# Neighbour sums in pairs in the scores' PSUM tiles, and the pieces of k over both other banks

## The chip, the cores and the metric

The kernel runs on one core of a Trainium2 chip. Times are device microseconds (us) of that core. Each time is a median of several executions. The traces' spans are some 2 us shorter than the times. Tables count batches from 1; the code counts them from 0. PE is TensorE's matmul, PEld its weight load, DVE VectorE, ACT ScalarE, POOL GpSimd.

## The reference

Two layers over x of 32 batches, 512 nodes, 512 features, all in fp32:

```
layer 0:  x = layernorm(x + deg * (x Wi' + b) + A (x Wj'))        A: the 512 x 512 graph, deg: its row sums
layer 1:  q, k, v = projections of x;  8 heads of 64
          x = layernorm(x + softmax(mask(q k' / 8)) v Wo' + bo)
```

## The kernel before

The program is a recorded list of pieces. While a batch n is in attention, eight steps each issue scores for four heads and a quarter of the keys, then the values (attention times v) of the step before, then other work: layer 0 of batch n+1, projections, the neighbour sums (`l0_gather`, x' A') of the batch after. Pieces are given weights and cut into the steps by these (`by_steps`).

PSUM has eight banks, and all are taken: one bank each for `mma` and `mmb`, two for `ov`, and two `sc` tiles of two banks each.

```python
def mm_tile(bank):
    return psum.tile([P, 512], FT, name="mm" + bank, bufs=1)
def sc_tile():
    return psum.tile([P, 2, N], FT, name="sc", bufs=2)
...
def l0_gather(b, dc, bank, adjT=None):
    ...
    pm = mm_tile(bank)
    parts = SPLIT.pop((b, dc))                    # xhi, xlo: x in two parts of type fp32r
    for w in range(2):
        for jc in range(NC):
            nc.tensor.matmul(pm, parts[w][:, jc, :], adjR[:, jc, :], start=..., stop=...)
    nc.scalar.copy(AX_T[b][:, dc, :], pm)         # ACT takes it out of PSUM
    if adjT is None and dc + 2 < DC:
        split(b, dc + 2)                          # ACT cast, POOL subtraction
...
def base(b, half):                                # DVE: y += deg * b0, two SBUF inputs
    for ic in range(2 * half, 2 * half + 2):
        y = XT[b][:, ic, :]
        nc.vector.scalar_tensor_tensor(y, b0_r, deg_c[:, ic:ic + 1], y, op0=OP.mult, op1=OP.add)
...
def scores(b, hp, kc):
    ps = sc_tile()
    ...                                           # matmuls, exp on ACT in place
    nc.vector.tensor_tensor(e, ps, edge..., op=OP.mult)   # the mask: last reader of ps
```

A gather is eight matmuls of 512 columns in fp32r, a second number type of TensorE. A piece of k is four matmuls of 256 columns in fp32, into a bank that DVE then adds into k. The trace lists an fp32 matmul twice and an fp32r matmul once, so a piece of k shows as eight records, x8; it prints both types as f32.

## Time and profile before

| | before |
|---|---|
| time, median of 5 | 3709.78 us (3708.73 to 3709.93) |
| span in the trace | 3706.9 us |
| PE busy | 3665.2 us, 99% |
| DVE, POOL, ACT busy | 65%, 53%, 28% |
| one batch in attention, start to start | 113.43 us |
| first scores, from the span's start | 117.45 us |

PE is busy nearly throughout, so the kernel is as long as its chain of matmuls. A batch's duration is the difference between the starts of its first scores and those of the next batch, in the timeline of PE; it is the same within 0.01 us from batch 2 to batch 30.

### The profile page before, as it was taken

To read this page: it belongs to the slowest core of one execution; us is meant where nothing else is said; L and a number is where in the kernel's file an instruction comes from. 1 tells how busy PE (TensorE), PEld (TensorE's weight loads), DVE (VectorE), ACT (ScalarE), POOL (GpSimd) and SP (SyncE) were. 2 spreads that over 40 slices of the span, in tenths; PEclk is the share of its full clock that TensorE was granted. 3 is DMA by queue.
4 is the path that set the end of the run, shared out by engine and by line. 5 is a ranking of instruction groups with operands and counts; after the bars stand their busy time and mean duration, and the time that the engine had idled before them with its cause. 6 is when DMAs were issued, how large, how long until landed. Compare 5 with 4: busy or idle time off the path is not lost.

```text
span 3706.9 us, 49623 instructions
## 1 busy us (share of the span) xinstructions
PE 3665.2 (99%) x18458; PEld 2511.4 (68%) x18458; DVE 2396.9 (65%) x3139; ACT 1029.1 (28%) x1482; POOL 1946.5 (53%) x1986
## 2 busy tenths in 40 slices
PE   8999999999999999999999999999999999999997
PEld 5666666666676767676666767676767666666763
DVE  4566766666666666666666666666666666666666
ACT  2222232222322222323233222222232332222322
POOL 3465545555455564455554555644555545556443
PEclk9999999999999999999999999999999999999999
DMA  7444556455555545554555544455545555445541
GB/s 250 125 126 133 151 151 162 124 141 138 152 159 145 128 135 150 153 160 120 141 142 154 159 141 130 134 151 157 157 122 139 141 159 157 137 132 137 151 131 44
DMA packets 797174, 530.02 MB, mean 143 GB/s; under 512 B 530433, under 2 KB 611841, under 8 KB 796929
## 3 DMA queue, kind: packets, MB, share of 16 engines
q1 hardware_dynamic: 780384, 494.78, 49.4%
q10 hardware_dynamic: 16320, 31.46, 2.3%
q8 instruction: 151, 2.47, 0.3%
q14 instruction: 95, 0.77, 0.1%
q0 software_dynamic: 224, 0.53, 0.0%
HBM read 453.25 MB, written 73.40 MB: 142 GB/s over the span
## 4 chain that ended last, share of the span: by engine, by line
PE 96%; DVE 1%; SPq 1%; POOL 1%; DMA 0%; issue 0%; ACT 0%; POOLq 0%; DVEq 0%; ACTq 0%
PE mma L427 31%; PE mmb L427 31%; PE sc L481 13%; PE ov L503 13%; PE mmb L325 3%; PE mma L325 3%; PE sc L513 2%; SPq L113 0%; DMA wv<-e 0%; DVE e L486 0%; DVE rl L522 0%; DVE st L289 0%; SPq L144 0%; PE sc L721 0%; SPq L166 0%
## 5 line engine op out<-in xcount | busy, mean ns | idle before, releaser
L485 ACT ACTIVATE sc<-sc 128x1024 f32<-128x1024 f32 x512 | 493.1, 1006 | 1538.4 <-PE sc L481 1532.2
L486 DVE TENSOR_TENSOR e<-sc,edge 128x1024 f32<-128x1024 f32 x512 | 602.5, 1218 | 211.4 <-ACT sc L485 180.4
L427 PE MATMUL mmb<-ring,big 128*128 128x256 f32 x3144 | 733.7, 382 | 3.1 <-issue 3.1
L427 PE MATMUL mma<-ring,big 128*128 128x256 f32 x3112 | 724.5, 381 | 3.9 <-ACT p L434 2.8
L427 PEld LDWEIGHTS mmb<-ring,big 128*128 128x128 f32 x3144 | 593.7, 190 | 134.1 <-issue 30.2
L427 PEld LDWEIGHTS mma<-ring,big 128*128 128x128 f32 x3112 | 585.7, 190 | 135.6 <-issue 27.0
L481 PE MATMUL sc<-q,k 64*128 64x512 f32 x2048 | 509.7, 616 | 0.0
L396 POOL TENSOR_TENSOR big<-big 128x512 f32<-128x512 f32 x376 | 493.1, 1339 | 29.3 <-ACT big L354 10.1
L503 PE MATMUL ov<-e,v 128*32 128x512 f32 x4096 | 494.0, 600 | 3.6 <-DVE oT L538 3.6
L492 POOL TENSOR_TENSOR es<-e 128x1024 f32<-128x1024 f32 x128 | 301.0, 2364 | 346.0 <-DVE e L486 346.0
L427 PE MATMUL mma<-big,ring 128*128 128x256 f32 x1808 | 431.5, 382 | 3.2 <-DVE k L465 3.2
L427 PE MATMUL mmb<-big,ring 128*128 128x256 f32 x1776 | 422.7, 381 | 0.0
L291 POOL TENSOR_SCALAR mv<-mv 128x1 f32<-128x1 f32 x256 | 51.0, 199 | 672.5 <-DVE mv L290 660.0
L427 PEld LDWEIGHTS mma<-big,ring 128*128 128x128 f32 x1808 | 341.0, 190 | 76.8 <-issue 25.1
L427 PEld LDWEIGHTS mmb<-big,ring 128*128 128x128 f32 x1776 | 334.5, 190 | 72.0 <-issue 25.1
L503 PEld LDWEIGHTS ov<-e,v 128*32 128x32 f32 x4096 | 107.1, 109 | 351.6 <-issue 321.7
L204 POOL TENSOR_TENSOR xlo<-xh,xhi 128x512 fp32r<-128x512 f32 x128 | 164.0, 1294 | 337.3 <-ACT xhi L203 337.2
L481 PEld LDWEIGHTS sc<-q,k 64*128 64x128 f32 x2048 | 176.5, 186 | 208.4 <-issue 205.4
L340 POOL TENSOR_TENSOR big<-big,deg_r 128x512 f32<-128x512 f32 x124 | 174.0, 1404 | 266.5 <-DVE big L339 266.5
L494 DVE TENSOR_TENSOR es<-es,e 128x1024 f32<-128x1024 f32 x251 | 307.7, 1227 | 0.0
L445 DVE TENSOR_TENSOR xh<-xh,mma 128x512 f32<-128x512 f32 x186 | 126.7, 681 | 269.7 <-PE mma L427 269.7
L445 DVE TENSOR_TENSOR xh<-xh,mmb 128x512 f32<-128x512 f32 x186 | 126.7, 681 | 262.6 <-PE mmb L427 262.6
(147 smaller groups left out, 3659.5 us busy)
## 6 DMA issues: line engine op xcount, KB each, us to landing
ring<-wo SPq DMA_DIRECT2D x217, 256.0 KB, 2.8
ring<-wq SPq DMA_DIRECT2D x160, 256.0 KB, 3.9
ring<-wv SPq DMA_DIRECT2D x160, 256.0 KB, 3.3
ring<-wk SPq DMA_DIRECT2D x160, 256.0 KB, 3.4
ring<-wi SPq DMA_DIRECT2D x155, 256.0 KB, 2.7
ring<-wj SPq DMA_DIRECT2D x155, 256.0 KB, 2.6
xh<-in_x_dram SPq DMA_DIRECT2D x32, 1024.0 KB, 5.5
xa<-in_x_dram SPq DMA_DIRECT2D x124, 256.0 KB, 3.9
```

Source lines behind the costliest of these rows:

```text
L204: nc.gpsimd.tensor_sub(lo, xs, hi.bitcast(FT))
L325: nc.tensor.matmul(pm, parts[w][:, jc, :], adjR[:, jc, :], start=(w == 0 and jc == 0), stop=(w == 1 and jc == NC - 1))
L340: nc.gpsimd.tensor_tensor(XD[b][:, dc, :], XD[b][:, dc, :], deg_r, op=OP.mult)
L396: nc.gpsimd.tensor_tensor(dst, p, q, op=OP.subtract)
L427: nc.tensor.matmul(pm[:, c * Q:(c + 1) * Q], lhs, rhs, start=first, stop=(kc == 1 and n == len(terms) - 1), skip_group_check=True)
L445: nc.vector.tensor_tensor(d, d, pm, op=OP.add)
L481: nc.tensor.matmul(ps[:, s, :], KT[b, hp // 2][r, hp % 2, kc * P:(kc + 1) * P], QT[b, hp // 2][r, hp % 2, :], start=True, stop=True)
L485: nc.scalar.activation(ps, ps, AF.Exp, scale=QSCALE)
L486: nc.vector.tensor_tensor(e, ps, edge[:, kc:kc + 1, :].to_broadcast([P, 2, N]), op=OP.mult)
L492: nc.gpsimd.tensor_add(ES[i], E[i, 0], E[i, 1])
L494: (eng or nc.vector).tensor_add(ES[i], ES[i], E[i, kc])
L503: nc.tensor.matmul(PV[g][r][32 * h:32 * h + 32, :], V[b][:, kc, c0:c0 + 32], E[h // 2, kc][:, h % 2, :], start=(kc == 0), stop=(kc == NC - 1))
```

## The change

Its intent: put two neighbour sums behind one another, in the two halves of one scores tile, so that their bank is free and the pieces of k can alternate between two banks.

```diff
-        pm = mm_tile(bank)
+        if bank == "sc":
+            if dc % 2 == 0:
+                OPEN["gather"] = sc_tile()
+            pm = OPEN["gather"][:, dc % 2, :]
+        else:
+            pm = mm_tile(bank)
...
-        g = [(GA, l0_gather, n, dc, A) for dc in range(DC)]
-        k = [pc("k", n - 1, i, K) for i in LATE]
-        res = []
-        for i in range(DC):
-            res += g[i:i + 1] + k[i:i + 1] + [z(l0_turn, n, i)]
-            if i in (1, 2):
-                res += [z(base, n, i - 1)]
-            if n == 1 and i in (1, 3):
-                res += [z(combine, "wo", nc.vector, i // 2)]
-            if i == 1:
-                res += [z(combos, TX, n, xq, (1,)), z(combos, TA, n, aq, (1,))]
+        g = [(GA, l0_gather, n, dc, "sc") for dc in range(DC)]
+        k = {i: pc("k", n - 1, i, A if i in (5, 3) else K) for i in LATE}
+        wo = [z(combine, "wo", nc.vector, i) for i in range(2)] if n == 1 else [z(base, n, 0), z(base, n, 1)]
+        res = [g[0], g[1], k[5]] if n == 1 else [k[5], g[0], g[1]]
+        res += [z(l0_turn, n, 0), k[6], z(l0_turn, n, 1), z(combos, TX, n, xq, (1,)), z(combos, TA, n, aq, (1,)), k[3], wo[0],
+                k[7], wo[1], g[2], g[3], z(l0_turn, n, 2), z(l0_turn, n, 3)]
+        if n == 1:
+            res += [z(base, n, 0), z(base, n, 1)]
```

(The return that follows is only broken over its lines in another way.)

More of the change, by code (lines that the diff above doesn't have):

```diff
@@ L571, in phase_a @@
         xq, aq = lambda j, m: quarter(XD[n], j, m), lambda j, m: quarter(AX_T[n], j, m)
-        g = [(GA, l0_gather, n, dc, A) for dc in range(DC)]
-        k = [pc("k", n - 1, i, K) for i in LATE]
-        res = []
-        for i in range(DC):
-            res += g[i:i + 1] + k[i:i + 1] + [z(l0_turn, n, i)]
-            if i in (1, 2):
-                res += [z(base, n, i - 1)]
-            if n == 1 and i in (1, 3):
-                res += [z(combine, "wo", nc.vector, i // 2)]
-            if i == 1:
-                res += [z(combos, TX, n, xq, (1,)), z(combos, TA, n, aq, (1,))]
+        g = [(GA, l0_gather, n, dc, "sc") for dc in range(DC)]
[6 more added lines that the diff above has]
+            res += [z(base, n, 0), z(base, n, 1)]
         return res + [z(combos, TX, n, xq, (2,)), z(combos, TA, n, aq, (2,)),
-                      z(combos, TX, n, xq, (3, 4)), z(combos, TA, n, aq, (3, 4)),
-                      pc("l0", n, 1, A), k[4]]
+                      z(combos, TX, n, xq, (3, 4)), z(combos, TA, n, aq, (3, 4)), pc("l0", n, 1, A), k[4]]
     def first():
```

## The prediction

> **What bounds the kernel now.** I read the page from the top: busy shares, then the chain that ended last.
>
> ```profile
> PE 3665.2 (99%) x18458; PEld 2511.4 (68%) x18458; DVE 2396.9 (65%) x3139; ACT 1029.1 (28%) x1482; POOL 1946.5 (53%) x1986
> ...
> PE 96%; DVE 1%; SPq 1%; POOL 1%; DMA 0%; issue 0%; ACT 0%; POOLq 0%; DVEq 0%; ACTq 0%
> ```
>
> TensorE (PE) is busy for all but 3706.9 - 3665.2 = 41.7 us of the span, and 96% of the last chain is matmuls. The chain in order of time repeats its entries every 113.43 us (1008.76, 1122.19, 1235.62): one batch, with the same pattern each time. So there is almost no idle PE to win. What can change is how long the matmuls take where they change from one kind to another, or a new wait in each batch. I therefore went to the timeline of PE, over the stretch where the changed code runs.
>
> ```profile
> 986.45 1.99 PE L481 MATMUL sc<-q,k 64*128 64x512 f32 x8
> 988.37 1.92 PE L503 MATMUL ov<-e,v 128*32 128x512 f32 x16
> 990.23 1.21 PE L325 MATMUL mmb<-adjR,xhi 128*128 128x512 f32 x4
> 991.27 1.07 PE L325 MATMUL mmb<-adjR,xlo 128*128 128x512 f32 x4
> 992.18 1.89 PE L427 MATMUL mma<-big,ring 128*128 128x256 f32 x8
> 993.72 1.28 PE L325 MATMUL mmb<-adjR,xhi 128*128 128x512 f32 x4
> 994.84 1.08 PE L325 MATMUL mmb<-adjR,xlo 128*128 128x512 f32 x4
> 995.75 1.89 PE L427 MATMUL mma<-big,ring 128*128 128x256 f32 x8
> ...
> 1001.14 1.99 PE L481 MATMUL sc<-q,k 64*128 64x512 f32 x8
> 1003.06 1.92 PE L503 MATMUL ov<-e,v 128*32 128x512 f32 x16
> 1004.91 1.21 PE L325 MATMUL mmb<-adjR,xhi 128*128 128x512 f32 x4
> 1005.96 1.07 PE L325 MATMUL mmb<-adjR,xlo 128*128 128x512 f32 x4
> 1006.87 1.89 PE L427 MATMUL mma<-big,ring 128*128 128x256 f32 x8
> 1008.59 3.62 PE L427 MATMUL mmb<-ring,big 128*128 128x256 f32 x16
> 1012.05 1.89 PE L427 MATMUL mma<-big,ring 128*128 128x256 f32 x8
> ```
>
> The first column is the start, so differences of starts are what each piece costs. A neighbour sum (gather) is the pair of L325 lines, a piece of k is eight L427 matmuls. From 1006.87 to 1008.59 eight plain matmuls take 1.72 us, from 1008.59 to 1012.05 sixteen take 3.46 us: 0.216 us each, 1.73 for eight. A gather has eight matmuls too, but k piece and gather together, 992.18 to 995.75, take 3.57 us, not 3.46: going into the fp32r form and out again costs about 0.12 us. A gather right behind the values (L503) takes 1.96 us, 0.23 over. A k piece there would take 1.83 us: 0.10 over (I read that behind other values lines, 1061.54 to 1063.37).
>
> The second view is the same stretch on DVE and POOL, in front of the scores that start at 1001.14:
>
> ```profile
> 999.31 1.27 POOL L340 TENSOR_TENSOR big<-big,deg_r 128x512 f32<-128x512 f32 x1
> 999.39 3.42 DVE L345 SCALAR_TENSOR_TENSOR xh<-b_r,deg_c,xh 128x512 f32<-128x512 f32 x2 [0.21 <-POOL xlo L204]
> 1000.66 3.28 POOL L396 TENSOR_TENSOR big<-big 128x512 f32<-128x512 f32 x2
> ...
> 1002.72 0.68 DVE L465 TENSOR_TENSOR k<-mma,k 128x512 f32<-128x512 f32 x1
> 1003.36 2.35 DVE L486 TENSOR_TENSOR e<-sc,edge 128x1024 f32<-128x1024 f32 x2
> ```
>
> The two base additions (L345) take 1.7 us each here, beside POOL; by themselves such an instruction takes 0.70 us (the group's minimum 705 ns, median 1746). They delay L465 and then the masking e<-sc (L486), which is the last reader of a scores tile.
>
> **What the Trainium skill says.** "SBUF — State Buffer", section "Who interferes with whom": a DVE instruction with two SBUF inputs and a GpSimd instruction that reads SBUF share an interface, and the second to issue blocks until the first has finished. The trace agrees: 0.70 against 1.75 us, and L345 ends about 0.55 us after the POOL operation that it overlapped (999.31 + 1.27 = 1000.58; the first L345 ends at 1001.13). "Perfetto Trace Analysis", section "Matmuls": independent groups should rotate through PSUM banks so that the eviction of one overlaps the next. The kernel before does that by alternating gather (one bank) and k piece (the other), and its PE shows no gap there; so the change cannot win hidden evictions. "TensorE: Matmul & The Clock Gate", section "Step-by-step: what each phase is for": a stream costs its N columns per matmul, with the drain hidden. The 0.216 us for 256 columns agree with two passes of 256 at 2.4 GHz plus 2.5 ns, which is my estimate from that page.
>
> **The change part by part.** Instructions are neither added nor removed: the program order has 2054 rows on PE before and after. (a) A batch had four separate gathers, each between other work; now there are two pairs, each in the two halves of a scores tile. (b) Pieces 5 and 3 of k go to the bank that the gathers left, 6, 7, 4 stay in the other. The built order of one batch is now: scores, values, k5, g0 g1, k6, k3, k7, scores, values, g2 g3, 16 matmuls of l0, k4. (c) On DVE the first base now stands between the additions of k3 and k7, where before it stood ahead of one k addition; the second base still comes behind the masks.
>
> PE, from the first values to the next batch's scores. Before: 1013.87 - 988.37 = 25.50 us. After, from the same starts: values 1.85, k5 1.64 (the first fp32r matmul starts 0.19 earlier than a plain one would), first pair 1.12 + 0.86 + 0.86 + 0.91 = 3.75, k6 1.73, k3 1.73, k7 1.82 (to scores), scores 1.92, values 1.85, second pair 1.96 + 1.73 = 3.69, l0 3.46, k4 1.82. Sum 25.26. The gain is 0.24 us a batch, two changes of kind fewer. Thirty batches have this under attention, and the preparation of batch 1 has it once more: 31 x 0.24 = 7.4 us.
>
> New waits. The first pair needs the third scores tile, that is the first of the two of this step, after its mask. With k5 ahead of it there is 1.6 us to spare: no wait. The second pair follows the values directly, 3.77 us (1.92 + 1.85) after the scores start, so the first mask of the step must have ended by then. Before, it ended at 1003.36 + 1.22 = 1004.58, which is 3.44 after the scores: 0.33 to spare. After, I work it out with the scores of the first step at 0. k6 runs 9.16 to 10.89, k3 to 12.62, k7 to 14.35, second scores at 14.43. POOL: the copy of g1 at 9.37, its fp32r cast 0.48 later, xlo 0.70 later at 10.55 to 11.85, then the two L340 to 13.1 and 14.34, then L396. DVE: addition of k3 at 12.82 (0.2 after its matmuls), base at 13.44, in the middle of the second L340. Its first half ends at 14.34 + 0.55 = 14.89, POOL's next ends at 16.02 (it starts late by 0.32), the second half at 16.57; addition of k7 from 16.49, mask from 17.12 to 18.34. That is 3.91 after the scores, 0.47 later than before. Waiters on this mask (L513) started 0.05 after it, so the gather would start at 3.96 in place of 3.77: 0.19 us lost a batch, 30 x 0.19 = 5.7 us.
>
> Net: -7.4 + 5.7 = -1.7 us; 3709.2 - 1.7 = about 3707.5. I take 3707, as the wait may be partly hidden.
>
> **The rivals.** (1) No wait at all: the base falls between POOL operations, or the lock is granted otherwise. Then the whole 7.4 us stay: 3702. For it speaks that 0.19 us rests on a chain of ten durations; against it that POOL has a queue of four operations just there. (2) A longer wait: one more POOL operation comes before the base, and the mask ends a whole L340 (1.27 us) less some slack later. A wait of 0.5 us a batch is 30 x 0.5 = 15 less 7.4: about 3717. (3) k7 waits for the DVE read of k6, which now has only k3 between them (1.73 us) in place of a gather and more: the two additions of k6 start at 11.1 and end at 11.99, k7 starts at 12.62, 0.6 to spare; only a late DVE makes this a wait. (4) DMA: three k pieces now take their weights within 5.2 us. Seven ring tiles and 2.7 to 3.9 us to landing make this safe.
>
> **Range and chances.** All of these are under 0.5% of the time, and 2% is 74 us, or 2.4 us a batch, which none of them reaches. The range goes from no wait with a slightly larger gain (3700) to a wait of some 0.4 us a batch (3714). Faster by over 2%: 0.01; within: 0.98; slower: 0.01.
>
> **What would show it.** In the PE timeline of after: the first pair should stand between two k pieces at about 3.75 us from start to next start; the batch should repeat every 113.43 - 0.24 + 0.19 = 113.4 us. The gather behind the second values should be named as waiting for the mask e<-sc, with the start some 3.9 to 4.0 us after the scores; if it stands at 3.77, rival 1 is right. The base pair on DVE should still take about 3.1 us beside POOL; with 1.4 the lock argument has failed. A wait of k7's weights on the k addition would be rival 3. I would be wrong altogether if another engine or the ring got gaps over 2 us in each batch.

## More of the kernel before

`combine("wo", ...)` is five DVE operations, done once per program, for n == 1 in the code, which is ahead of the first scores.

## The result

The changed kernel took 3771.76 us (median of 5, 3770.03 to 3773.24), 62 us more. The ratio to before is 1.0169, 95% interval 1.0155 to 1.0183; a ratio here is the mean time of one kernel's fast runs over that of the other's in the same rounds, so not quite the quotient of the medians. The results are correct. The prediction of 3707 us, 3700 to 3714, was wrong.

The page of the changed kernel, busy shares and the last chain by engine:

```profile
PE 3685.2 (98%) x18458; PEld 2505.1 (66%) x18458; DVE 2357.2 (63%) x3139; ACT 1029.3 (27%) x1482; POOL 1933.4 (51%) x1986
...
PE 95%; DVE 1%; ACT 1%; SPq 1%; POOL 1%; issue 0%; DMA 0%; DVEq 0%; POOLq 0%; ACTq 0%
```

The span is 63.0 us longer (3769.9 against 3706.9), but PE's busy time only 20 us. PE now idles 43 us more, and ACT has come into the chain with 1%, where it had 0%. The view of waits, with the total in us, the number of waits and the longest, names them:

```profile
PEld sc L331 <- ACT big L337: 66.2, 60, 1.1
...
PE sc L331 <- ACT big L337: 40.5, 60, 0.7
```

L331 is the gather's matmul and L337 the copy of a gather out of PSUM. Sixty gathers wait for a copy; in the kernel before three did, 0.7 us together (PE), all in the first batch's layer 0. PEld (66.2 us) and PE (40.5 us) describe one and the same wait, so they aren't added. The timeline of PE shows where it stands (start, duration, and in brackets the idle time before):

```profile
1011.76 1.28 PE L331 MATMUL sc<-adjR,xhi 128*128 128x512 f32 x4
1012.88 1.07 PE L331 MATMUL sc<-adjR,xlo 128*128 128x512 f32 x4
1014.63 1.21 PE L331 MATMUL sc<-adjR,xhi 128*128 128x512 f32 x4 [0.68 <-ACT big L337]
1015.67 1.07 PE L331 MATMUL sc<-adjR,xlo 128*128 128x512 f32 x4
1016.58 1.89 PE L433 MATMUL mma<-big,ring 128*128 128x256 f32 x8
...
1021.86 1.99 PE L487 MATMUL sc<-q,k 64*128 64x512 f32 x8
1023.77 1.92 PE L509 MATMUL ov<-e,v 128*32 128x512 f32 x16
1025.69 1.20 PE L331 MATMUL sc<-adjR,xhi 128*128 128x512 f32 x4
1026.73 1.08 PE L331 MATMUL sc<-adjR,xlo 128*128 128x512 f32 x4
1028.49 1.19 PE L331 MATMUL sc<-adjR,xhi 128*128 128x512 f32 x4 [0.68 <-ACT big L337]
1029.52 1.08 PE L331 MATMUL sc<-adjR,xlo 128*128 128x512 f32 x4
1030.44 3.61 PE L433 MATMUL mmb<-ring,big 128*128 128x256 f32 x16
```

The second gather of each pair starts when the copy of the first is done: in ACT's timeline

```profile
1013.99 0.59 ACT L337 COPY big<-sc 128x512 f32<-128x512 f32 x1 [4.55 <-PE sc L331]
```

ends at 1014.58, and the gather starts at 1014.63. A pair takes 4.82 us (1011.76 to 1016.58) and 4.75 us (1025.69 to 1030.44). The first scores of the batches give where the 63 us are. All rows are differences of starts in PE's timeline:

| stretch | before | after | difference |
|---|---|---|---|
| start of the span to the first scores | 117.45 | 114.04 | -3.41 |
| batch 1 in attention | 102.39 | 113.88 | +11.49 |
| batches 2 to 30 (29 x 113.43, 29 x 115.40) | 3289.56 | 3346.54 | +56.98 |
| batch 31 | 107.47 | 105.86 | -1.61 |
| batch 32 and the end | 90.03 | 89.58 | -0.45 |
| sum | | | +63.0 |

Three things need explaining: 1.97 us in each batch, 11.5 us in batch 1, and a gain of 3.4 us ahead of the first scores. (The 1.6 us of batch 31 were not followed up: late_whole, below, has the same 105.86 us, the other runs 107.3 to 107.6.) For batch 1, the timeline of PE shows the scores of a step torn apart:

```profile
191.58 1.07 PE L331 MATMUL sc<-adjR,xlo 128*128 128x512 f32 x4
192.58 1.13 PE L487 MATMUL sc<-q,k 64*128 64x512 f32 x4
196.15 1.78 PE L487 MATMUL sc<-q,k 64*128 64x512 f32 x4 [2.44 <-DVE e L492]
...
200.70 1.21 PE L331 MATMUL sc<-adjR,xhi 128*128 128x512 f32 x4
```

Here a pair has been cut by the end of a step: one gather before the scores, the other behind them, while their tile stays open. The second scores then wait for the mask (L492) of the first. The batch's other cut pair does the same and waits 4.45 us (at 215.36).

### The profile page after: what moved, and what is told of

Same layout as the page of the kernel before. It is cut to its first block, busy times and chain, and to the rows that moved or that the text cites.

```text
span 3769.9 us, 49539 instructions
## 1 busy us (share of the span) xinstructions
PE 3685.2 (98%) x18458; PEld 2505.1 (66%) x18458; DVE 2357.2 (63%) x3139; ACT 1029.3 (27%) x1482; POOL 1933.4 (51%) x1986
## 4 chain that ended last, share of the span: by engine, by line
PE 95%; DVE 1%; ACT 1%; SPq 1%; POOL 1%; issue 0%; DMA 0%; DVEq 0%; POOLq 0%; ACTq 0%
PE mmb L433 31%; PE mma L433 31%; PE sc L487 13%; PE ov L509 12%; PE sc L331 7%; PE sc L519 2%; ACT big L337 1%; SPq L113 0%; DVE e L492 0%; DMA wv<-e 0%; DVE rl L528 0%; SPq L144 0%; DVE st L289 0%; PE sc L723 0%; SPq L166 0%
## 5 line engine op out<-in xcount | busy, mean ns | idle before, releaser
L492 DVE TENSOR_TENSOR e<-sc,edge 128x1024 f32<-128x1024 f32 x512 | 601.8, 1216 | 216.0 <-ACT sc L491 185.1
L346 POOL TENSOR_TENSOR big<-big,deg_r 128x512 f32<-128x512 f32 x124 | 156.7, 1286 | 188.8 <-DVE big L345 188.8
```

Source lines behind the costliest of these rows:

```text
L346: nc.gpsimd.tensor_tensor(XD[b][:, dc, :], XD[b][:, dc, :], deg_r, op=OP.mult)
L492: nc.vector.tensor_tensor(e, ps, edge[:, kc:kc + 1, :].to_broadcast([P, 2, N]), op=OP.mult)
```

## The experiments

Theory T: the program keeps the order between reads and later writes by tile, not by half. The copy out of the first half was recorded before the matmuls into the second, so these wait for it, though they touch another bank. Rivals: R1, the gather's own operands (cast on ACT, remainder on POOL) are late; R2, the new order and banks of k cost the time. The first four runs shared nine runs of the kernel before, median 3707.80 us, and the second four shared nine others, median 3708.59 us, on another chip. All kernels gave correct results.

T can also be read from the programs. The recorded kernels were built again, without a run, and each wait value was followed to the instruction that reaches it. In the changed kernel all 62 second gathers of a pair wait, at their first matmul, for the copy L337 of the first half of their own tile. In late_copies and one_copy these 62 wait for the cast L203 in that place, and in own_tiles 60 wait for a mask and two for a cast. So the wait is one that the program sets, and it goes by the tile.

### late_copies: the copies behind the pair

```diff
-        nc.scalar.copy(AX_T[b][:, dc, :], pm)
+        if bank == "sc" and dc % 2 == 0:
+            OPEN["first"] = pm
+        else:
+            if bank == "sc":
+                nc.scalar.copy(AX_T[b][:, dc - 1, :], OPEN["first"])
+            nc.scalar.copy(AX_T[b][:, dc, :], pm)
```

> The changed kernel, with one thing moved: the ACT copy of the first gather of a pair is recorded after the matmuls of the second gather, so both copies of a pair stand together. No instruction is added or removed. Theory T (the second gather waits for the copy of the first because both halves are one tile, and the order between a read and a later write is kept by tile): the gap of 0.68 us before each second gather goes, a pair takes 3.7 us from start to next start in place of 4.8, and the time is the prediction's 3707 us (3702 to 3710), 62 us below the changed kernel. Rival R1 (the second gather's own operands come late: the cast on ACT or the rest on POOL): the gap stays, about 3770 us. Rival R2 (the other bank order of k costs it): about 3770 us as well.

Measured: 3711.19 us (3709.09 to 3712.06), ratio 1.0007 (0.9993 to 1.0021); the loss is gone but for some 3 us. A batch takes 113.40 us, as against 115.40. The second pair in PE's timeline:

```profile
1008.11 1.92 PE L514 MATMUL ov<-e,v 128*32 128x512 f32 x16
1009.97 1.20 PE L331 MATMUL sc<-adjR,xhi 128*128 128x512 f32 x4
1011.00 1.08 PE L331 MATMUL sc<-adjR,xlo 128*128 128x512 f32 x4
1011.91 1.07 PE L331 MATMUL sc<-adjR,xhi 128*128 128x512 f32 x4
1012.83 1.08 PE L331 MATMUL sc<-adjR,xlo 128*128 128x512 f32 x4
1013.75 3.61 PE L438 MATMUL mmb<-ring,big 128*128 128x256 f32 x16
```

The gap is gone: 3.78 us for the pair in place of 4.75. No instruction was added or removed; only the place of one copy in the recorded order differs, and k's order is that of the changed kernel. That contradicts R1 and R2. The time lay a little above the expected range of 3702 to 3710, because batch 1 still takes 113.28 us; late_whole, below, is about that.

### one_copy: one copy for the pair

```diff
-        nc.scalar.copy(AX_T[b][:, dc, :], pm)
+        if bank != "sc":
+            nc.scalar.copy(AX_T[b][:, dc, :], pm)
+        elif dc % 2 == 1:
+            nc.scalar.copy(AX_T[b][:, dc - 1:dc + 1, :], OPEN["gather"])
```

> The changed kernel, with one ACT copy of 128x1024 for the pair in place of two of 128x512. T: no gap, as in late_copies, and ACT is busy some 0.2 us less per pair (two copies take 2 x 0.59 us; a 128x1024 activation takes 1.0): 3707 us (3702 to 3710). R1 and R2: about 3770 us.

Measured: 3728.52 us (3725.91 to 3729.10), ratio 1.0053 (1.0039 to 1.0066). The wait for the copy is gone, but I had expected 3707. A batch takes 113.90 us, and the half microsecond above late_copies stands in front of the third gather:

```profile
1012.49 1.92 PE L512 MATMUL ov<-e,v 128*32 128x512 f32 x16
1014.85 1.19 PE L331 MATMUL sc<-adjR,xhi 128*128 128x512 f32 x4 [0.43 <-DVE e L495]
```

That is the wait for the mask which the prediction had worked out for the changed kernel. It came out longer because the two base additions took 3.50 us here, against 3.06 us in the changed kernel. In late_copies, with the base in the same place, they took 2.42 us and the gather did not wait. Why one long copy shifts the work beside them is not shown. one_copy_base tests the base's part.

### own_tiles: a scores tile for each gather

```diff
-            if dc % 2 == 0:
-                OPEN["gather"] = sc_tile()
-            pm = OPEN["gather"][:, dc % 2, :]
+            pm = sc_tile()[:, 0, :]
```

> The changed kernel, with each gather in a scores tile of its own (first half), copies where they were: the copy of the first gather runs beside the matmuls of the second, in another tile. T: no wait for the copy; the second gather of the second pair now needs the second mask of the step, which ends about 5.1 us after the scores start, and it would start at 5.8: no new wait. 3707 us (3702 to 3712). If a running ACT read anywhere in the scores' banks held up the gather (not the tile), the gap would stay: about 3770 us. R1: 3770 us.

Measured: 3705.27 us (3703.58 to 3706.66), ratio 0.9991 (0.9978 to 1.0005), as T expected. The copy of the first gather is where it was and runs beside the second's matmuls, now in another tile, and the second gather does not wait. So an ACT read in the scores' banks was no hindrance by itself. A batch takes 113.46 us. The third gather starts 1.92 us after the values (1000.01 to 1001.93), 0.06 later than in late_copies: the wait for the mask, small.

### apart: the halves kept, the pairs undone

```diff
-        res = [g[0], g[1], k[5]] if n == 1 else [k[5], g[0], g[1]]
-        res += [l0_turn 0, k[6], l0_turn 1, combos..., k[3], wo[0], k[7], wo[1], g[2], g[3], l0_turn 2, l0_turn 3]
+        res = [k[5], g[0], l0_turn 0, k[6], g[1], l0_turn 1, combos..., k[3], k[7], g[2], *wo, l0_turn 2, l0_turn 3]
-        return res + [combos..., l0 piece 1, k[4]]
+        return res + [l0 piece 1, g[3], combos..., k[4]]
```

(shortened: the calls without their arguments)

> The gathers stay in the halves of scores tiles and k over both banks, but the pairs are pulled apart: k5 g0 k6 g1 k3 k7, then g2, the 16 matmuls of l0, g3, k4; the base additions stand behind g2, so that they delay no mask. T: the copy is hidden behind the piece between, as before the change; as many changes of kind as in the kernel before, so its time: 3709 us (3706 to 3713). If the room (the scores tile) or the order of k costs the time and not the neighbourhood of the two gathers: 3730 to 3770 us.

Measured: 3713.59 us (3713.43 to 3714.68), ratio 1.0014 (0.9999 to 1.0030), 0.6 us above T's range. From batch 2 on it is the kernel before to the hundredth: 113.43 us a batch. So neither the room of the scores nor the order of k costs anything; it is two gathers of one tile with nothing between them. The 6 us above the kernel before are the 11.1 us that batch 1 takes longer (113.48 us against 102.39, where pairs are cut by the steps again), less 4.9 us gained ahead of the first scores.

### late_whole: no pair cut by a step

late_copies, but the gathers with b == 2 in the code (the third batch), the ones that are made while batch 1 of the table is in attention, have tiles of their own and their copies at once.

```diff
-            if dc % 2 == 0:
+            if dc % 2 == 0 or b == 2:
                 OPEN["gather"] = sc_tile()
...
-        if bank == "sc" and dc % 2 == 0:
+        if bank == "sc" and dc % 2 == 0 and b != 2:
             OPEN["first"] = pm
         else:
-            if bank == "sc":
+            if bank == "sc" and b != 2:
```

> late_copies, with own tiles for the gathers of batch 2 alone, whose pairs are cut by the end of a step (first gather, scores, second gather). Theory (a tile held open over the scores leaves these one tile, so that the second scores of the step wait for the mask of the first): the two waits of 2.44 and 4.10 us go, the first batch under attention takes 104 us in place of 113.3, and the time is 3709.4 - 9 = 3700 us (3699 to 3703). Rival (these waits are DVE's or POOL's load in the first batch): as late_copies, 3709 us.

Measured: 3704.14 us (3702.46 to 3705.82), ratio 0.9989 (0.9975 to 1.0003). Batch 1 takes 104.22 us in place of 113.28: 9.06 less, as expected. The time lay 1 us above the expected range; one later batch in the trace is 0.8 us longer, which was not followed up. The rival falls: the load of DVE and POOL is the same, and only the tile held open is gone.

### own_tiles_base and one_copy_base: the base behind the masks

```diff
-                k[3], wo[0], k[7], wo[1], g[2], g[3], ...
+                k[3], *wo[:1 if n == 1 else 0], k[7], *wo[1:2 if n == 1 else 0], g[2], *wo[2 if n == 1 else 0:], g[3], ...
```

> own_tiles, with both base additions recorded behind the third gather, that is behind the masks of the step, from batch 2 on. Theory (the base on DVE beside POOL delays the mask, and the gather behind it): the small wait of the third gather (it starts 1.92 us after the values in place of 1.85) goes, 113.46 us a batch becomes 113.40, and in the first batch under attention the wait of 1.76 us for the mask goes too: about 1.7 + 1.8 us less, 3701 to 3702 us. Rival (the third gather waits for the mask for another reason, such as the mask's own length): as own_tiles, 3705 us.

> one_copy with the base additions behind the third gather. In one_copy a batch takes 113.90 us, as the third gather waits 0.43 us for the mask. Theory: that wait goes, 113.40 us a batch, 29 x 0.5 = 14.5 us less: 3712 us. Rival (the long copy itself holds ACT or the tile and causes the wait): as one_copy, 3727 us.

Measured: own_tiles_base 3703.75 us (3700.15 to 3704.74), ratio 0.9984 (0.9970 to 0.9997); one_copy_base 3710.72 us (3708.87 to 3712.08), ratio 1.0005 (0.9992 to 1.0019); expected were 3701 to 3702 and 3712. The usual batch takes 113.40 us in both (own_tiles_base has four batches that are 0.15 to 0.44 us longer, which I did not follow up). For one_copy that is 0.50 us a batch and, with batch 1 (109.36 us in place of 113.86), some 18 us in all. So the wait for the mask needs the base additions ahead of it; the long copy alone does not cause it. The base alone does not either: late_copies has it there, with short copies, and no such wait. In own_tiles_base batch 1 takes 102.39 us, as in the kernel before, where own_tiles took 104.21.

### before_wo: the kernel before, with the wo combinations moved

```diff
-            if n == 1 and i in (1, 3):
-                res += [z(combine, "wo", nc.vector, i // 2)]
+            if n == 1 and i == 3:
+                res += [z(combine, "wo", nc.vector, 0), z(combine, "wo", nc.vector, 1)]
```

> The kernel before, with one thing: the five operations on DVE that form the combinations of wo, once per program, stand behind the last neighbour sum and not in two parts among the k pieces. Theory (the changed kernel gains 3.4 to 5.5 us ahead of the first scores because these operations no longer stand between a k piece and its addition): the wait of 3.17 us at the fourth k piece goes, first scores at 114 us in place of 117.45, 3703.5 us. Rival (the gain ahead of the first scores comes from the gathers leaving the bank): as before, 3707 us.

Measured: 3703.37 us (3700.92 to 3703.59), ratio 0.9983 (0.9970 to 0.9997). In the kernel before, PE's timeline has this ahead of the first scores:

```profile
104.40 1.08 PE L325 MATMUL mmb<-adjR,xlo 128*128 128x512 f32 x4
108.66 3.14 PE L427 MATMUL mma<-big,ring 128*128 128x256 f32 x8 [3.17 <-DVE k L465]
```

A piece of k waits for the addition of an earlier one, because that addition stands in DVE's queue behind the first three wo operations, of which this is the last:

```profile
107.31 0.69 DVE L254 TENSOR_TENSOR e<-xh,e 128x512 f32<-128x512 f32 x1
107.92 0.68 DVE L465 TENSOR_TENSOR k<-mma,k 128x512 f32<-128x512 f32 x1
```

In before_wo the same two pieces are:

```profile
102.76 1.07 PE L325 MATMUL mmb<-adjR,xlo 128*128 128x512 f32 x4
103.67 1.89 PE L427 MATMUL mma<-big,ring 128*128 128x256 f32 x8
```

The wait is gone, and the first scores come earlier than the expected 114 us. From the first gather to the first scores the kernel before takes 24.87 us (92.58 to 117.45), before_wo 19.74 (90.93 to 110.67), and the changed kernel 21.65 (92.39 to 114.04), its two waits for copies included. So such a gain comes from the order of DVE's work alone, and needs neither the pairs nor the scores' tiles; the changed kernel, too, has no wait for L471, the addition into k, there. (What lies before the first gather varies by some 1.7 us between these traces, and nothing follows from that. Three later batches of before_wo are 0.2 to 0.6 us longer, which was not followed up.)

## Why the prediction was wrong

**The step that failed**: "the first pair 1.12 + 0.86 + 0.86 + 0.91 = 3.75", and "second pair 1.96 + 1.73 = 3.69". I counted a pair as sixteen matmuls in one stream, taking the halves of a tile for independent. Under "New waits" I asked only what the first gather of each pair needs ("1.6 us to spare: no wait", which held), and never what the second needs. Measured, a pair waits: 4.82 and 4.75 us. Without the wait, in one_copy and late_copies, they are 3.86 (1001.44 to 1005.30) and 3.78 us. That makes 0.96 + 0.97 = 1.93 us of the 1.97 us a batch; the rest is a mask wait of 0.06 us less a gain of 0.03, both below. late_copies and own_tiles remove it by the recorded order alone and by the tile alone. The built order lists the second gather with a wait on ACT, which I took for its cast; late_copies, which does not stall there, has a wait on ACT listed too. The wait's value tells them apart: followed to its instruction, it is the cast L203 in late_copies and the copy L337 in the changed kernel. The question to ask was which earlier instruction reads the tile that is about to be written.

**The gain was mis-sized.** 0.24 us a batch was predicted from two changes of kind fewer; late_copies, which has the pairs and no waits, gains 0.03 (113.43 to 113.40). I had put the 0.12 us that a gather cost above a k piece down to the change between fp32 and fp32r. But inside the unbroken fp32r stream of late_copies four matmuls take 0.91 or 0.92 us (1011.91, 1012.83, 1013.75), 0.229 each. The 0.216 I used belonged to another kind: to a record of k's fp32 matmuls of 256 columns. Eight of the gather's matmuls are 0.10 us more than eight such records, with no change of kind between them. So 3.75 and 3.69 should have been 3.86 and 3.78, and the pairing saves almost nothing.

**Batch 1 was left out.** I multiplied one batch by 31 without looking whether the steps cut the list alike everywhere. In batch 1 the cut falls inside the pairs, and a tile stays open across the scores: +11.5 us in the changed kernel. late_whole shows 9.06 us for it (in late_copies). Moving the base took another 1.8 us from batch 1 (own_tiles to own_tiles_base). Added across kernels, which makes it an estimate, some 0.6 us of the 11.5 stay unassigned.

**The start was left out too**: -3.4 us. before_wo shows that the order of DVE's work is enough for it.

**What was right.** The lock between DVE and POOL and the wait for the mask are there. In the changed kernel:

```profile
1020.84 3.06 DVE L351 SCALAR_TENSOR_TENSOR xh<-b_r,deg_c,xh 128x512 f32<-128x512 f32 x2
1023.83 0.68 DVE L471 TENSOR_TENSOR k<-mma,k 128x512 f32<-128x512 f32 x1
1024.43 2.34 DVE L492 TENSOR_TENSOR e<-sc,edge 128x1024 f32<-128x1024 f32 x2
```

The base pair takes 3.06 us (predicted 3.1), as the Trainium skill's page "SBUF — State Buffer", section "Who interferes with whom", lets one expect of a DVE instruction with two SBUF inputs beside GpSimd; a single one took from 0.70 us to 1.78 us in the kernel before. The first mask ends at 1024.43 + 1.21 = 1025.64, which is 3.78 us after the scores (1021.86); predicted was 3.91. The gather's weight load starts 0.05 us after it, as predicted. The gather starts 1.92 us after the values, against 1.86 in late_copies. The wait is some 0.06 us, not 0.19: the mechanism was right, a chain of ten durations was 0.13 off. Rivals 3 and 4 did not come up as waits in the views used; rival 1, no wait at all, was wrong, but nearly right in size. None of my rivals held a wait between the two gathers of a pair, which is what happened. The chance of 0.98 for "within 2%" stood, at 1.7%, but by luck: it rested on every effect being under 0.5%.

No version here beats the kernel before by more than 0.2%: own_tiles_base and before_wo lie at 0.9984 and 0.9983 with intervals just below 1, and what they gain lies almost all ahead of the first scores.

## What to carry to other kernels

Before two pieces of work are put next to each other in parts of one tile, find the reader of the first part and ask whether the second has to wait for it; the built program's waits, followed to their instructions, tell. Record the reads behind both writes, or give each its own tile. Check a repeating pattern also in the first and last rounds, where a cut can fall elsewhere. And before a saving is ascribed to a transition, measure the rate inside the unbroken stream.

## What the Trainium skill lacked or had wrong

- "Perfetto Trace Analysis", section "Matmuls", advises to rotate independent groups through different PSUM banks, so that the copy out of one overlaps the next. It lacks that two banks did not give this here while they were halves of one tile and the copy of the first was recorded ahead of the matmuls of the second: 0.96 us a pair, some 58 us over the sixty pairs that stalled (an estimate, 60 x 0.96). No page that I read has it.
- "TensorE: Matmul & The Clock Gate", section "Back-to-back issue gap", gives N / 2.4 + 2.5 ns for an isolated matmul, 216 ns for 512 columns, and about 131 ns for a stream of matmuls with weight loads; it names no number type. In the unbroken stream here 128x512 fp32r matmuls with a weight load each ran at 229 ns. A record of a 128x256 fp32 matmul took 216 ns, where the formula gives 109 for 256 columns, and each such matmul stands in the trace as two records.
- The same page, section "LDWEIGHTS (loading the stationary operand)", gives P / 1.2, 107 ns for 128 columns; for fp32 and fp32r the weight loads here took 186 to 190 ns in the trace, and those of 32 columns (L503) 109 ns, where the formula gives 27.
